# A list-scheduled transformer kernel: the first norm's small steps on VectorE, two routing steps for either engine, new lengths and due times in the layout

## The chip, the cores and the metric

The kernel runs on one core of a Trainium2 chip. That core has five engines with queues of their own: TensorE (matmul; PE in the profile, its weight loads PEld), VectorE (DVE), ScalarE (ACT), GpSimd (POOL) and SyncE (SP), which here only issues transfers. Each engine works through its own list of instructions in the order in which the program wrote them, and waits at semaphores for the others. The metric is the device time of one launch in microseconds; the time before is the median of three runs.

## What is computed

The reference is a stack of four gated layers over x of 16 batches x 128 tokens x 128 features, with a context of 77 rows a batch. Each layer adds a cross attention and a feed-forward part, each behind a layer norm and a tanh gate. Only what the change touches is shown in detail:

```python
def _layernorm(x, axis=-1, eps=1e-05):
    m = jnp.mean(x, axis=axis, keepdims=True)
    v = jnp.var(x, axis=axis, keepdims=True)
    return (x - m) / jnp.sqrt(v + eps)
...
    x = x + jnp.tanh(g_xattn[0]) * _L0_xattn_ref(_layernorm(x, axis=-1), ctx_1024, ctx_1024, ...)
    x = x + jnp.tanh(g_ffn[0]) * _L0_ffn_ref(_layernorm(x, axis=-1), L0_ffn_gate_w, L0_ffn_w1, L0_ffn_w2)
...
# layer 0's router, per token over E = 8 experts
select_prefix = jnp.arange(E)[None, :] <= k_idx[:, None]
R_sorted = jnp.where(select_prefix, p_sorted - rank, jnp.full_like(p_sorted, -1000000000.0))
...
tok_order = jnp.argsort(-R, axis=0)      # an expert keeps its 256 best tokens by R
```

Layers 0 and 1 attend with 16 heads of 8 features (layer 0 with a mask, and its weights are multiplied by a given matrix after the softmax), layer 2 with 16 heads of 64, layer 3 with 8 heads of 64. The feed-forward parts are a routed mixture of 8 experts, a dense layer with a second norm, a layer with 8-bit rounding, and a mixture that takes the best expert of each token.

## The kernel before

The tokens are worked on in four groups of four batches (`NG`, `GB`), a batch being 128 tokens on the 128 partitions. A group's x lies in SBUF throughout. Layer 0's attention goes group by group, eight units of half a batch each: scores on TensorE, the row maximum and the difference on VectorE (`less_max`, L632 and L634), exp on ScalarE (L839), the product with the given matrix on GpSimd or VectorE (`weighted`, L856), sums on VectorE (L844), transposes and the product with the values on TensorE. In layers 2 and 3 `weigh` (L995) takes the place of `weighted`.

**The order is laid out by a planner in the program.** Nothing is issued where it is written. Each piece of work is handed to `add(at, engine, cost, fn, reads, writes, new)`: a due time `at`, the engine or the engines that may do it, a cost in microseconds for each, and the keys it reads and writes. `Work.layout` (from L216) then runs a list scheduling over all pieces: whenever an engine is idle by its clock it takes the ready piece with the smallest due time. A piece that may go on two engines goes to the one that would finish it first by the costs, VectorE being charged 0.5 more (`SLACK`). The instructions are then written in this order, so costs and due times decide every engine's queue and nothing else. `NUDGES` (from L76) is a list of 582 triples: first piece, how many pieces, and hundredths of a microsecond added to their due times. `FLEX` is ScalarE or VectorE; `WEIGH` and `SIDE` are GpSimd or VectorE.

**The norm** (`norm`, L482) has five pieces: `stats` on VectorE (L491, four instructions), `moments` on GpSimd (L498 to L503, six instructions on 128x4 or 128x8 elements), `guess` on ScalarE (L508 and L510, logarithm and exponential), `newton` on GpSimd (L514 to L520, five instructions), and `scaled` on ScalarE (L526) or VectorE (L528), four instructions, one for each batch. `transposed` (L610) needs all four. The very first norm, of group 0 in layer 0, stands ahead of everything that TensorE does with x. At the start GpSimd also makes the identity, the head mask, `billion`, four cleared `vz` tiles (L1171) and the mask penalties `pen` (L1190, or on VectorE).

**Layer 0's routing** (`route_part`, L1525 to L1607) follows for each group once its logits are there: softmax, `before1` (L1562 to L1565) and `before2` (L1569 to L1577), which find an expert's rank and the mass ahead of it and make R from them, `spread` (L1582), which copies R sixteen times side by side, four transposes and their eviction into `RB`. All of its VectorE pieces were on VectorE alone. After the last group seven rounds of counting over `RB` (L1715) find each expert's cut.

Of the kernel before, what the change touches and what calls it, by code (L numbers as in the profile page):

```python
# [18 lines left out]
ALU = mybir.AluOpType  # L19
# [3 lines left out]
P = 128  # L23
B = 16
D = 128
SK = 77
NG = 4
GB = B // NG
GT = GB * P
GK = GB * SK  # L30
E = 8
# [28 lines left out]
WEIGH, WEIGH_COST = ("POOL", "DVE"), (1.3, 0.85)  # L60
SIDE, SIDE_COST = ("POOL", "DVE"), (1.3, 0.75)
# [12 lines left out]

NUDGES = (
    (206, 1, 230), (1755, 1, 143), (2153, 1, -200), (2640, 4, 268), (963, 1, -150), (960, 4, -257), (1701, 1, 117), (1797, 3,  # L76
    -30), (989, 1, -212), (1726, 8, -153), (2228, 4, 172), (2164, 2, -283), (1712, 1, -267), (1001, 1, -283), (1670, 6,
    -289), (1652, 1, -189), (813, 1, -237), (164, 8, -58), (162, 2, -260), (879, 6, 267), (1136, 1, -206), (141, 4, -145),
    (130, 1, 220), (738, 6, -165), (2242, 4, -104), (961, 1, -103), (2244, 8, -295), (1770, 2, 104), (488, 8, 333), (1339, 1,
    65), (466, 8, 69), (611, 4, 133), (1771, 1, -214), (65, 1, -226), (137, 4, -273), (2126, 1, -231), (567, 1, -156), (991,  # L80
    1, -231), (2046, 4, 47), (1919, 6, -283), (2452, 4, 299), (2195, 1, 100), (689, 1, -177), (1805, 2, 116), (332, 8, -352),
    (337, 8, -46), (956, 3, -22), (749, 8, -114), (2053, 8, 58), (2559, 1, -190), (501, 8, 217), (2655, 8, -72), (1935, 1,
    -263), (1015, 1, -100), (2403, 1, -88), (2766, 8, 120), (18, 8, 217), (399, 1, -14), (1548, 4, -46), (1542, 6, -252),
    (2445, 4, -44), (397, 8, 38), (849, 8, -70), (961, 1, -99), (1914, 2, -52), (1530, 4, -250), (869, 4, 264), (392, 1,
    156), (2068, 6, -52), (852, 4, 92), (1693, 2, -62), (991, 3, -232), (611, 8, 89), (869, 1, -276), (801, 1, 281), (2196,
    8, -30), (2416, 6, -273), (2216, 1, -248), (867, 5, -264), (2514, 5, -30), (798, 1, -157), (2351, 2, -317), (2685, 8,
    -69), (1474, 1, -91), (2385, 1, 256), (1690, 1, -24), (2175, 1, 121), (2054, 4, -47), (2514, 4, 127), (1485, 8, 274),
    (392, 2, 72), (2542, 6, -186), (1806, 8, 89), (987, 5, -196), (2633, 3, -250), (492, 8, -236), (406, 1, -183), (1838, 4,
    -210), (2352, 1, 274), (2199, 1, -277), (1610, 6, -212), (2547, 1, 242), (1723, 4, 60), (1676, 1, 271), (2059, 8, -270),
    (268, 8, -210), (1753, 8, 42), (2631, 2, -107), (1547, 1, -182), (1579, 4, 19), (377, 1, -73), (2080, 1, -38), (465, 1,  # L90
    -122), (2636, 3, 278), (995, 3, -161), (1571, 8, -123), (751, 1, -281), (249, 4, -311), (2634, 8, -121), (854, 6, 175),
    (798, 1, 75), (2614, 8, -397), (2289, 1, -240), (1009, 1, -99), (2536, 4, -99), (1299, 1, -270), (1024, 4, -270), (741,
    1, -114), (2480, 1, -296), (2417, 2, -257), (761, 1, -284), (2254, 2, -218), (971, 2, -251), (1011, 4, -314), (2837, 8,
    252), (1936, 4, 186), (2111, 8, -333), (1853, 1, 135), (600, 8, -33), (1839, 1, -241), (1855, 5, -100), (940, 1, -191),
    (769, 5, -205), (2002, 8, -31), (781, 4, -32), (756, 1, 62), (1072, 8, 12), (755, 2, -156), (2636, 2, 106), (1983, 8,
    -341), (1339, 1, -80), (1386, 1, -266), (859, 1, -136), (1416, 8, 137), (46, 4, 380), (756, 1, 143), (758, 1, -131),
    (1391, 2, 150), (2561, 1, -293), (940, 1, -187), (1841, 4, -270), (1507, 1, 86), (1946, 8, 10), (981, 1, -279), (446, 6,
    -301), (2680, 1, -210), (1864, 1, 190), (737, 2, -81), (1015, 1, 241), (1552, 3, 189), (2717, 4, -126), (18, 5, -237),
    (1001, 2, 288), (1022, 1, 163), (2195, 1, -59), (2536, 5, 258), (2458, 4, -80), (2490, 1, -296), (2494, 6, -198), (1560,
    4, -287), (1911, 5, -16), (864, 1, -297), (149, 3, 221), (1876, 4, 273), (1434, 4, -304), (2206, 3, -140), (41, 8, 260),  # L100
    (1443, 8, -98), (2206, 8, 75), (2039, 5, -256), (2046, 1, -229), (922, 1, -228), (985, 1, -170), (2074, 1, -269), (1418,
    4, -275), (2793, 5, -298), (2718, 4, -126), (1507, 1, -302), (869, 6, 233), (2206, 1, -48), (2034, 1, -65), (2068, 1,
    -220), (1851, 1, -301), (748, 4, 118), (1397, 8, 143), (1507, 1, 286), (1514, 1, -260), (375, 1, -253), (985, 1, -152),
    (2206, 1, -42), (2252, 1, -231), (1746, 8, 119), (2306, 1, 78), (1467, 6, -111), (1633, 1, 72), (1952, 1, -186), (981, 1,
    172), (411, 2, -92), (559, 8, 123), (397, 4, -18), (1219, 1, -151), (2480, 2, 127), (852, 1, -203), (1613, 2, 294),
    (2670, 8, -326), (2256, 1, -242), (953, 1, -194), (1058, 8, 100), (1952, 1, -49), (532, 1, -164), (1048, 4, -80), (1054,
    8, -91), (741, 1, -138), (2249, 8, 400), (987, 6, -205), (367, 6, -265), (803, 8, 294), (1414, 2, -267), (2897, 8, -243),
    (2492, 3, -282), (963, 1, 115), (1633, 1, -57), (1509, 1, -97), (1041, 2, 306), (806, 1, -238), (2008, 1, -88), (975, 1,
    -260), (920, 8, -208), (258, 8, -230), (491, 8, -48), (874, 1, -300), (607, 2, -81), (945, 1, -271), (789, 3, -171),
    (460, 1, 24), (791, 4, 298), (258, 2, 336), (741, 1, -71), (689, 1, -288), (2897, 4, 388), (1005, 1, -266), (959, 1,  # L110
    -21), (857, 1, 92), (431, 3, -191), (934, 1, -104), (801, 1, 296), (851, 4, -164), (854, 4, -222), (1851, 1, -94), (993,
    5, -152), (2101, 1, -233), (971, 1, 279), (972, 2, -204), (254, 1, -202), (1940, 8, -90), (869, 1, 75), (973, 1, -112),
    (1794, 3, -141), (2592, 4, -114), (973, 4, -248), (859, 6, -286), (2470, 1, -271), (1570, 2, -115), (533, 4, 282), (961,
    1, -279), (46, 8, -174), (969, 1, -122), (1612, 3, -61), (971, 2, -134), (2242, 5, 240), (2114, 8, -331), (1575, 4,
    -325), (2897, 4, -181), (2095, 4, -171), (276, 1, 275), (969, 1, -211), (1042, 1, -131), (1896, 4, 108), (969, 8, -121),
    (763, 1, -263), (2099, 3, -38), (2206, 4, -65), (1000, 4, -204), (2357, 4, 299), (579, 4, -325), (662, 3, -236), (2856,
    8, -367), (484, 8, 218), (2161, 1, -159), (223, 2, -98), (1570, 1, -262), (244, 8, -158), (222, 8, 52), (2175, 4, 50),
    (1503, 4, -114), (2473, 8, 89), (1843, 8, 137), (2215, 6, -274), (139, 1, 191), (1004, 6, -159), (748, 1, -271), (1838,
    4, -140), (2849, 1, 134), (999, 1, -226), (985, 4, -245), (2798, 5, -220), (922, 4, -286), (1052, 2, 119), (928, 5,
    -300), (981, 1, -222), (740, 8, -110), (1612, 4, -84), (1015, 2, -88), (996, 8, -105), (44, 8, -95), (2461, 5, 205),  # L120
    (1502, 4, -117), (2221, 4, -226), (485, 4, -357), (297, 4, -110), (1050, 4, -134), (2813, 1, -122), (1709, 1, -130),
    (1613, 8, 134), (2448, 8, 230), (969, 1, -243), (1004, 4, -257), (763, 1, -222), (2778, 4, 99), (2470, 8, 194), (689, 1,
    -221), (852, 4, -204), (741, 1, -194), (981, 1, -125), (1202, 6, -239), (894, 1, -144), (2159, 1, -243), (1609, 8, -138),
    (1466, 4, -384), (961, 1, -177), (991, 3, -168), (2474, 1, -277), (1057, 3, -180), (502, 1, -127), (2777, 5, 273), (1895,
    4, -78), (965, 5, -74), (995, 1, -230), (854, 4, -281), (154, 2, 382), (2206, 2, 85), (753, 2, -288), (2215, 6, -253),
    (969, 8, -361), (745, 4, 83), (974, 5, -239), (923, 6, -261), (983, 1, -186), (879, 1, 71), (625, 1, -169), (981, 1,
    -132), (140, 5, -185), (1802, 4, 47), (481, 8, 253), (2304, 2, -132), (1801, 5, -82), (2388, 6, 296), (743, 4, -136),
    (983, 6, 97), (872, 6, 146), (949, 5, -17), (865, 5, 90), (925, 5, -181), (136, 5, -180), (778, 1, -78), (803, 1, -263),
    (368, 1, 208), (2837, 8, 354), (1228, 1, 115), (2206, 1, -65), (1058, 1, -151), (793, 1, -302), (643, 1, 276), (2205, 3,
# [27 lines left out]
class Work:  # L157
# [50 lines left out]
    def nudged(self):  # L208

        due = [n["at"] for n in self.nodes]  # L210
        for first, count, hundredths in NUDGES:
            for i in range(first, min(len(due), first + count)):
                due[i] += hundredths / 100.0
# [1865 lines left out]
```

## Time and profile before

| what | us |
|---|---|
| median of three runs | 663.42 (663.17, 663.42, 665.4) |
| the profiled execution | 666.49 |
| its span, first to last instruction | 664.8 |
| L634 DVE difference, 112 instructions | 89.5 busy, 0.799 each |
| L632 DVE maximum, 112 | 87.4 busy, 0.780 each |
| L995 on POOL, 34 / on DVE, 14 | 1.216 / 0.899 each |
| L856 on POOL, 26 / on DVE, 6 | 1.387 / 1.031 each |
| L526 on ACT into xn, 92 / L528 on DVE, 20 | 0.486 / 0.551 each |
| L498 on POOL, 39 | 0.203 each |

The span lies inside the execution's time; what is around it is 1.7 us. An engine is busy while it computes; issuing transfers and waiting do not count. TensorE's mean granted clock is 0.976 of full speed. The kernel reads and writes 117.5 MB by DMA, at a mean of 177 GB/s.

### The profile page before, as it was taken

The page shows a single profiled execution, that of the slowest core. Times are in us where ns is not written, and L with a number is a line of the kernel's source. Part 1 is how long each engine was busy: PE and PEld are TensorE (multiplying, and loading weights), DVE is VectorE, ACT ScalarE, POOL GpSimd, SP SyncE. Part 2 cuts the span into 40 slices and gives each one's busy share as a digit, 9 for nine tenths or more (in the row PEclk, how much of TensorE's full clock was granted, in tenths as well). Part 3 has the DMA queues.
Part 4 walks back from the last instruction along what each step waited for, and adds up shares of the span by engine and source line. Part 5 has one row for each costly group of instructions (what it writes and reads, how often), then busy time and mean ns, then how long its engine had stood idle before and what let it go on. Part 6 is the DMA issues. An engine that isn't in the chain of part 4 may idle for free.

```text
span 664.8 us, 16370 instructions
## 1 busy us (share of the span) xinstructions
PE 604.2 (91%) x5795; PEld 435.4 (65%) x5795; DVE 524.9 (79%) x1224; ACT 427.2 (64%) x1131; POOL 305.8 (46%) x750
## 2 busy tenths in 40 slices
PE   3988998899999999988989999999999998799795
PEld 2555565565546778655646776687767776689795
DVE  3699999884675347999998998979999999878342
ACT  3545758577766656686687867647686758356463
POOL 8659445351000027624362735445445347645554
PEclk9888999999999999998999999999999999799898
DMA  8972473557445565489592757569964432666473
GB/s 228 272 233 68 150 183 110 150 165 207 144 131 159 160 187 144 140 239 296 160 269 88 217 169 227 188 175 315 292 178 130 122 98 83 198 180 181 125 225 84
DMA packets 169178, 117.47 MB, mean 177 GB/s; under 512 B 12649, under 2 KB 159984, under 8 KB 169098
## 3 DMA queue, kind: packets, MB, share of 16 engines
q1 hardware_dynamic: 166650, 112.55, 59.6%
q0 software_dynamic: 1728, 3.17, 1.3%
q8 instruction: 46, 0.75, 0.5%
q10 hardware_dynamic: 720, 0.71, 0.4%
q14 instruction: 34, 0.28, 0.1%
HBM read 61.43 MB, written 55.89 MB: 176 GB/s over the span
## 4 chain that ended last, share of the span: by engine, by line
PE 29%; DVE 13%; ACT 7%; POOL 7%; issue 2%; DMA 1%; another core or an unknown queue 1%; DVEq 0%; ACTq 0%; POOLq 0%
PE T L650 4%; PE h_ps L1927 4%; PE y L1001 4%; PE y L1942 3%; DVE pr L634 3%; PE q_ps L931 3%; DVE mx L632 2%; PE y L1062 2%; POOL pw L995 2%; PE h_ps L1041 2%; PE S L975 1%; DVE sb L988 1%; ACT xn L526 1%; PE O L885 1%; DVE ln_st L491 1%
## 5 line engine op out<-in xcount | busy, mean ns | idle before, releaser
L634 DVE TENSOR_TENSOR pr<-S,mx 128x616 f32<-128x616 f32 x112 | 89.5, 799 | 6.7
L632 DVE TENSOR_REDUCE mx<-S 128x8 f32<-128x616 f32 x112 | 87.4, 780 | 4.8 <-PE S L824 4.0
L650 PE MATMUL T<-ident,pw 128*128 128x128 f32 (+1 forms) x400 | 63.0, 284 | 6.5 <-POOL pw L995 4.3
L463 ACT COPY pT<-T 128x384 f32<-128x384 f32 x107 | 50.5, 479 | 26.6 <-PE T L650 26.0
L995 POOL TENSOR_TENSOR pw<-pr,rinv 128x616 f32<-128x616 f32 x34 | 41.2, 1216 | 53.5 <-DVE rinv L990 10.4
L650 PEld LDWEIGHTS T<-ident,pw 128*128 128x128 f32 (+1 forms) x400 | 45.9, 142 | 29.1 <-issue 12.0
L1001 PEld LDWEIGHTS y<-v,pT 128*128 128x128 f32 (+1 forms) x480 | 57.8, 191 | 9.6 <-issue 4.0
L1001 PE MATMUL y<-v,pT 128*128 128x128 f32 (+1 forms) x480 | 62.1, 278 | 1.5 <-ACT pT L463 1.1
L839 ACT ACTIVATE pr<-pr 128x616 f32<-128x616 f32 x64 | 45.9, 720 | 20.3 <-DVE pr L634 20.1
L856 POOL TENSOR_TENSOR pw<-pr,gp 128x616 f32<-128x616 f32 x26 | 36.0, 1387 | 37.2 <-ACT pr L839 23.9
L1811 DVE SCALAR_TENSOR_TENSOR token<-y,sc,token 128x128 f32<-128x128 f32 x96 | 32.9, 349 | 24.2 <-PE y L1806 21.7
L844 DVE TENSOR_REDUCE ss<-pr 128x8 f32<-128x616 f32 x64 | 49.6, 781 | 1.3 <-ACT pr L839 1.1
L931 PE MATMUL q_ps<-xT,wq 128*128 128x512 f32 x96 | 49.5, 613 | 0.8 <-DVE token L693 0.5
L463 ACT COPY vs<-f_ps 122x512 f32<-122x512 f32 (+3 forms) x57 | 33.1, 584 | 24.3 <-PE f_ps L1486 22.6
L1951 POOL DMA_INDIRECT out_x<-bo,row x30 | 29.8, 994 | 30.0 <-DVE bo L1946 15.1
L526 ACT ACTIVATE xn<-token,ln_b,ln_r 128x128 f32<-128x128 f32 x92 | 37.8, 486 | 7.4 <-POOL ln_b L520 7.3
L984 ACT ACTIVATE pr<-pr 128x616 f32<-128x616 f32 x48 | 34.0, 718 | 12.5 <-DVE pr L634 7.9
L657 ACT COPY pT<-T 128x128 f32<-128x128 f32 x104 | 28.2, 271 | 17.5 <-PE T L650 15.7
L1486 PE MATMUL f_ps<-vz,ctxT 128*122 128x512 f32 (+3 forms) x80 | 39.2, 602 | 0.1
L988 DVE TENSOR_REDUCE sb<-pr 128x8 f32<-128x616 f32 x48 | 37.4, 779 | 1.5 <-ACT pr L984 1.5
L975 PE MATMUL S<-k,q 64*64 64x77 f32 x1536 | 35.8, 235 | 0.9 <-DVE pr L634 0.8
L975 PEld LDWEIGHTS S<-k,q 64*64 64x64 f32 x1536 | 31.1, 136 | 7.7 <-issue 3.5
(338 smaller groups left out, 1490.4 us busy)
## 6 DMA issues: line engine op xcount, KB each, us to landing
v<-folded SPq DMA_DIRECT2D x48, 320.0 KB
vx<-apart SPq DMA_DIRECT2D x32, 320.0 KB
apart<-vz SPq DMA_DIRECT2D x32, 308.0 KB
rowsA<-blank SPq DMA_DIRECT2D x15, 516.0 KB
rowsZ<-blank SPq DMA_DIRECT2D x15, 516.0 KB
kept<-ks SPq DMA_DIRECT2D x24, 308.0 KB
k<-kept SPq DMA_DIRECT2D x12, 616.0 KB
folded<-vs SPq DMA_DIRECT2D x21, 308.0 KB
```

The lines of the kernel that those rows point to most:

```text
L463: nc.scalar.copy(out, src)
L526: nc.scalar.activation(o[:, i, :], src()[:, i, :], AF.Identity, bias=mem["b"][:, i:i + 1], scale=mem["r"][:, i:i + 1])
L632: nc.vector.tensor_reduce(mx, S4, axis=AX.X, op=ALU.max)
L634: nc.vector.tensor_tensor(pr.rearrange("p (a c) k -> p a c k", a=2), S4, mx.unsqueeze(3).to_broadcast([P, 2, 4, SK]), ALU.subtract)
L650: nc.tensor.transpose(own[jkey][:n, c, :], flat[:, lo:lo + n], ident)
L839: nc.scalar.activation(own["pr", i, half], own["pr", i, half], AF.Exp)
L844: nc.vector.tensor_reduce(own["s", i][:, 8 * half:8 * half + 8], own["pr", i, half], axis=AX.X, op=ALU.add)
L931: nc.tensor.matmul(own["q_ps", c], lhsT=wq()[:, (c0 + c) * P:(c0 + c + 1) * P], rhs=mem["xT"], start=True, stop=True)
L975: nc.tensor.matmul(S[rows64, a, c * SK:(c + 1) * SK], lhsT=own["q"][at, c, i * P + 64 * b:i * P + 64 * b + 64], rhs=own["k"][at, c, i * SK ...
L988: nc.vector.tensor_reduce(s, own["pr", i], axis=AX.X, op=ALU.add)
L995: eng.tensor_tensor(own["pw", i], own["pr", i], own["rinv", i].unsqueeze(2).to_broadcast([P, 8, SK]), ALU.mult)
L1001: nc.tensor.matmul(own["y", i], lhsT=own[u + (i, "pT", c // 3)][:n, c % 3, :], rhs=own["v", i][:n, c, :], start=(c == 0), stop=(c == 4))
```

## The change

Four things are done, in one diff.

The first norm (layer 0, group 0) gets `first=True`: its `moments` and `newton` run on VectorE with the same eleven instructions, and its scaling becomes two pieces of two batches each, one on ScalarE and one on VectorE; a piece without an instruction joins them. In all other norms only the costs change.

In `route_part` the second half of `before2` becomes a piece of its own, `before3`, which may run on GpSimd or VectorE, and so may `spread`. What were two instructions with a scalar and two tensors are three with one operation each, so that the piece has five instructions where there were four.

Costs in the layout are set anew for some pieces. The nudges are replaced as a whole, 597 in place of 582; 46 of them have a count of 0, which is a new form: it adds to the charge for taking the piece's second engine.

```diff
-WEIGH, WEIGH_COST = ("POOL", "DVE"), (1.3, 0.85)
-SIDE, SIDE_COST = ("POOL", "DVE"), (1.3, 0.75)
+WEIGH, WEIGH_COST = ("POOL", "DVE"), (1.25, 0.95)
+SIDE, SIDE_COST = ("POOL", "DVE"), (1.2, 1.2)
...
 NUDGES = (
...
@@ nudged, layout
-        due = [n["at"] for n in self.nodes]
+        due, odds = [n["at"] for n in self.nodes], [0.0] * len(self.nodes)
         for first, count, hundredths in NUDGES:
+            if count == 0:
+                odds[first] += hundredths / 100.0
             for i in range(first, min(len(due), first + count)):
                 due[i] += hundredths / 100.0
-        return due
+        return due, odds
...
+        second = [list(n["on"])[-1] for n in nodes]
+        slack = lambda i, e: SLACK.get(e, 0.0) + (odds[i] if e == second[i] else 0.0)
...
@@ norm
+        few = nc.vector if first else nc.gpsimd
...
-            nc.gpsimd.tensor_tensor(d, st[:, :, 1], st[:, :, 4], ALU.subtract)
+            few.tensor_tensor(d, st[:, :, 1], st[:, :, 4], ALU.subtract)
...
-        def scaled(e):
-            o = mem["o"] = out()
-            for i in range(GB):
+        def scaled(e, batches=range(GB)):
+            if "o" not in mem:
+                mem["o"] = out()
+            o = mem["o"]
+            for i in batches:
...
+        if first:
+            add(at, "DVE", 0.9, moments, writes=[ln])
+            act(at, 0.45, guess, writes=[ln])
+            add(at, "DVE", 0.7, newton, writes=[ln])
+            for n, e in enumerate(FLEX):
+                half = range(2 * n, 2 * n + 2)
+                add(at, e, 0.85, lambda e=e, half=half: scaled(e, half), reads=list(skeys) + [ln], writes=[okeys[0] + (n,)], new=() if n else new)
+            add(at, "NONE", 0.0, None, reads=[okeys[0] + (n,) for n in range(2)], writes=okeys)
+            return
...
-        add(at, FLEX, (1.6, 1.36), scaled, reads=list(skeys) + [ln], writes=okeys, new=new)
+        add(at, FLEX, (1.66, 1.75), scaled, reads=list(skeys) + [ln], writes=okeys, new=new)
...
-            add(at, FLEX, ((0.47, 0.55), (0.5, 0.45))[j], out, reads=[T], writes=[jkey])
+            add(at, FLEX, ((0.48, 0.55), (0.54, 0.55))[j], out, reads=[T], writes=[jkey])
...
-                    add(th + 0.1, ("POOL", "DVE"), (1.4, 0.85), weighted, reads=[prk, ("gp", g)], writes=[skey], new=[("pws", skey)])
+                    add(th + 0.1, ("POOL", "DVE"), (1.4, 1.15), weighted, reads=[prk, ("gp", g)], writes=[skey], new=[("pws", skey)])
...
@@ route_part
+        def before3(e):
+            eng = nc.gpsimd if e == "POOL" else nc.vector
+            rank, chosen = own["rank"], own["chosen"]
             R = f0["R"][:, gs, :]
-            nc.vector.scalar_tensor_tensor(R, rank, 1.0, pr(), op0=ALU.add, op1=ALU.subtract)
-            nc.vector.scalar_tensor_tensor(R, R, -1.0, chosen, op0=ALU.mult, op1=ALU.mult)
-            nc.vector.tensor_scalar(chosen, chosen, 1.0, 1e9, op0=ALU.subtract, op1=ALU.mult)
-            nc.vector.tensor_tensor(R, R, chosen, ALU.add)
+            eng.tensor_scalar(rank, rank, 1.0, None, op0=ALU.add)
+            eng.tensor_tensor(R, pr(), rank, ALU.subtract)
+            eng.tensor_tensor(R, R, chosen, ALU.mult)
+            eng.tensor_scalar(chosen, chosen, 1.0, 1e9, op0=ALU.subtract, op1=ALU.mult)
+            eng.tensor_tensor(R, R, chosen, ALU.add)
...
-        add(at, "DVE", 1.5, before1, reads=[key], writes=[key])
-        add(at, "DVE", 2.0, before2, reads=[key], writes=[key])
-        add(at, "DVE", 0.6, spread, reads=[key], writes=[kx], new=[("xn", kx)])
+        both = ("POOL", "DVE")
+        add(at, "DVE", 2.3, before1, reads=[key], writes=[key])
+        add(at, "DVE", 1.45, before2, reads=[key], writes=[key])
+        add(at, both, (1.2, 0.9), before3, reads=[key], writes=[key])
+        add(at, both, (0.9, 0.45), spread, reads=[key], writes=[kx], new=[("xn", kx)])
```

## The prediction

> **What bounds the kernel.** I read the page's first part, then busy time by stretch, then the timeline of the first 24 us, then the groups and timeline of the operations that the change touches.
>
> ```profile
> PE 604.2 (91%) x5795; PEld 435.4 (65%) x5795; DVE 524.9 (79%) x1224; ACT 427.2 (64%) x1131; POOL 305.8 (46%) x750
> ```
>
> TensorE is busy for 604.2 of 664.8 us, and the change takes no matmul away. So the question is what becomes of the 60.6 us in which TensorE idles. The next view is busy time in six stretches: start and end, length, then PE, PEld, DVE, ACT and POOL busy with their instruction counts, granted clock, DMA share, GB/s.
>
> ```profile
> 0.00:20.00 20.00, 8.66 (x24) 5.66 (x25) 6.51 (x21) 7.16 (x15) 17.16 (x55) 0.87 0.84 230
> 20.00:160.00 140.00, 126.23 (x1088) 79.72 (x1087) 125.12 (x264) 88.83 (x231) 73.30 (x136) 0.97 0.59 168
> 160.00:250.00 90.00, 90.00 (x371) 55.40 (x370) 47.57 (x121) 59.66 (x120) 7.14 (x24) 1.00 0.54 159
> 250.00:550.00 300.00, 285.32 (x3379) 206.97 (x3382) 274.85 (x583) 210.10 (x564) 144.22 (x409) 0.99 0.66 191
> 550.00:600.00 50.00, 41.28 (x491) 35.87 (x484) 41.45 (x128) 28.92 (x87) 29.92 (x70) 0.93 0.54 154
> 600.00:664.80 64.80, 52.67 (x458) 51.74 (x456) 29.38 (x110) 32.56 (x118) 34.05 (x62) 0.94 0.57 155
> ```
>
> TensorE's idle time is length less busy: 11.3 us before 20, 13.8 up to 160, none up to 250, 14.7 up to 550, 8.7 up to 600, and 12.1 at the end; 60.6 together. The reader is to see four regimes. At the start GpSimd is the full engine (17.16 of 20) while TensorE and VectorE wait. From 20 to 160 (layer 0's attention) VectorE is nearly full, 125.1 of 140. From 160 to 250 TensorE never stops. From 250 to 550 both are nearly full, 95% and 92%.
>
> The start, in order of time (start, length, engine, line, operation):
>
> ```profile
> 5.09 0.87 DVE L491 BATCH_NORM_STATS2 ln_st<-token 128x6 f32<-128x128 f32 x4 [5.09 <-DMA token<-in_x]
> 5.26 3.63 POOL L1171 MEMSET vz<- 128x1024 f32 x4
> ...
> 8.86 0.21 POOL L498 TENSOR_TENSOR ln_d<-ln_st 128x4 f32<-128x4 f32 x1
> ...
> 9.38 1.43 DVE L766 TENSOR_TENSOR kx<-ks,headmask 128x1232 f32<-128x1232 f32 x1
> 9.46 1.42 POOL L501 TENSOR_SCALAR ln_w<-ln_sq 128x4 f32<-128x4 f32 x1
> ...
> 12.67 1.50 POOL L514 TENSOR_TENSOR ln_t<-ln_r 128x4 f32<-128x4 f32 x1
> ...
> 15.32 1.65 ACT L526 ACTIVATE xn<-token,ln_b,ln_r 128x128 f32<-128x128 f32 x4 [3.28 <-POOL ln_b L520]
> ...
> 15.87 1.63 PE L610 MATMUL tp<-ident,xn 128*128 128x128 f32 x4 [4.88 <-ACT xn L526]
> ```
>
> The statistics are ready at 5.96, but GpSimd first clears vz and starts on them only at 8.86. Two of its four-column steps last 1.42 and 1.50 us where the other norms need 0.19 and 0.20, each under a VectorE kx of 1.43. The mask pen stands between them on GpSimd from 11.43 to 12.69. So xn is finished at 16.97, and VectorE meets its first score (L632) at 23.07. Before that VectorE has done only 7.6 us of work (2.37 up to 10, 4.13 up to 20, then 0.75 and 0.31).
>
> **Part A, the first norm.** Removed from GpSimd: 6 + 5 small steps. Added to VectorE: the same 11. Rows: routing's small steps of 128x32 (L1574 to L1577) last 0.18 to 0.19 and follow each other every 0.22 us. So ln_w is ready at 5.96 + 5 x 0.22 = 7.1. The guess on ScalarE (0.44 from 11.19 to 11.63) must wait for a table load that ends at 7.47, so r is there at 7.9. Five steps more, 1.1, and a hop: 9.1. Scaling is four pieces of 0.41 on ScalarE (1.65); now two there and two on VectorE at 0.34 (L528's median), side by side 0.85. So xn is done at 10.0 instead of 16.97: 7.0 earlier on the path. The wait for r now stands in VectorE's queue; behind it are the vz evictions (L788), the bias rows and kx, and kx is what the scores also need. VectorE's own load bounds the gain again: 7.6 us of earlier work plus 11 x 0.22 + 0.7 = 3.1 makes 10.7, which from 5.09 ends no sooner than 15.8, against 23.07: at most 7.3. The other end is 0: the landing times of the masks and of vx aren't shown, and DMA is busy at 0.84 of its share here. Against that end, vx is issued at 15.11 and first used at 29.71 with no wait seen. I take -5.5, nearer to the two bounds that agree on 7 than to 0, because kx and the vz evictions must share VectorE with the norm. Is an earlier start kept? Layer 0 is bound by VectorE, whose list from there on is unchanged, and the full TensorE of 160 to 250 only moves up with it. So yes, unless a transfer is late next.
>
> **Part B, routing steps.** Two steps of each group may go to GpSimd: R's last arithmetic (now five instructions, four before) and its spread.
>
> ```profile
> 76.50 1.66 DVE L1562 TENSOR_TENSOR tie<-r_pr 128x256 f32<-128x256 f32 x1
> ...
> 81.64 0.19 DVE L1577 TENSOR_TENSOR R<-R,chosen 128x32 f32<-128x32 f32 x1
> 81.74 0.35 DVE L693 SCALAR_TENSOR_TENSOR token<-y,tg,token 128x128 f32<-128x128 f32 x1
> 82.00 0.42 DVE L1582 COPY rx<-R 128x512 f32<-128x512 f32 x1
> ```
>
> On VectorE they cost 4 x 0.22 + 0.42 = 1.3 a group. Groups 0 to 2 lie in VectorE's full stretch, so at most 3.9 is saved. Group 3's (at 175) lies under the full TensorE and is worth nothing unless that cover goes. On GpSimd nothing of this form ran: its norm steps follow every 0.28 (L515 to L520), 5 x 0.28 = 1.4, and a 128x512 pass is 1.18 (L689), so 2.6, 1.3 more latency before the transposes; if group 3's is uncovered, +1.3. GpSimd has 73.3 of 140 busy, so its queue takes the step, but a weighting (L856, 1.39) may stand behind it. The fifth instruction adds 0.22 where VectorE keeps the step. I take -1.0, between -3.9 and +1.3, since the layout moves a step only where it expects VectorE to finish later.
>
> The row of tie above shows a price of such moves: 1.66 us against 0.42 in the other groups, just while GpSimd's L856 runs from 76.49 to 77.88. The Trainium skill, "SBUF — State Buffer", section "Who interferes with whom", says that a VectorE instruction with two SBUF inputs and a GpSimd instruction that reads SBUF take turns on a shared port pair for the whole instruction. As an estimate by that rule, every moved step can hold VectorE for its own length, 3 x 2.6 = 7.8 against 3.9 saved, so that the part would read +3.9 instead of -1.0 and the total 660.8.
>
> **Part C, the measured lengths.** They shift the choice of engine: VectorE's weighting becomes dearer (0.85 to 0.95 and to 1.15), its side passes 0.75 to 1.2, its scaling 1.36 to 1.75. The rows agree: L995 on VectorE has a mean of 0.899, L856 1.031, L528 0.551 a piece. Work that can leave: L995 12.6, L856 6.2, L528 9.8, side passes 2.8, 31.4 us in all on VectorE. It goes to engines with room (ScalarE 210 of 300, GpSimd 144 of 300 between 250 and 550) but lasts longer there: 1.22 for 0.80 on L995. The gain is bounded by TensorE's idle time, which is owed to many causes; the loss by latency, 14 x 0.42 = 5.9. I take -1.0, range -6 to +5.9: nearest is the row that says TensorE already runs at 95% there.
>
> **Part D, the due times.** All 582 nudges go and 597 others come, some of them on the choice of engine. The trace can't price an order that it doesn't contain. Bounds: all of TensorE's 14.7 idle us between 250 and 550 gone, or that whole stretch at the rate of its first 100 us (4.0 + 6.1 idle, so 30.5): +15.8. I take 0.
>
> The sum is -5.5 - 1.0 - 1.0 + 0 = -7.5. The profiled execution took 666.49 with a span of 664.8, so 1.7 lie around the span; the span should come to 657.3 and that execution to 659.0. Carried to the median of the runs, 663.42 (3.1 below the profiled execution), this is 655.9.
>
> **Rivals.** First, more than that: the truer lengths halve the idle time between 250 and 550, 7.3 more, 648.6. For it: VectorE's 92% there, so a lighter VectorE is felt. Against: the chain of waits there alternates between TensorE, VectorE and the others, and no wait stands out. Second, a start that is hidden anyway: DMA share 0.91 from 10 to 40 holds masks or vx back, A is 0, and 661.4 is left, no change that shows. For it: that share. Against: no TensorE wait on a transfer between 6.5 and 600. Third, slower: the new order makes the L1 to L3 stretch, 250 to 550, wait for GpSimd's longer passes; at the rate of its first 100 us it costs +15.8, so 671.7. It cancels all gains from +7.5 and shows as a loss from +10.8. For it: TensorE's transposes already wait 4.3 us for GpSimd's pw, and the old order is fitted to these queues. Against: that engine is half idle.
>
> **How the numbers follow.** Forecast 0.47, the larger gain 0.18, hidden start 0.15, slower order 0.20. Faster by over 0.5% (under 660.1) is 0.65, within 0.5% 0.15, slower (over 666.7) 0.20; half a per cent is about what runs of this kernel can tell, 663.17 to 665.4. The forecast's own range is 651 to 660. The range for 8 in 10 reaches to the larger gain's value less a little, 646, and into the slower case, 668.
>
> **What would show it.** A: L498 to L520 on VectorE before 10, the first xn transposes near 10 to 11, the first L632 near 17 to 18, no 4.9 us TensorE wait for xn. B: rx and R's steps on GpSimd in groups 0 to 2. C: fewer than 14 L995, 6 L856 and 20 L528 instructions on VectorE, its busy sum below 520. D: TensorE idle between 250 and 550 near 14.7. The prediction is wrong if the first L632 is not before 21, or if the early start is there and idle time of 250 to 550 or of the end grows by more than it.

## The result and the profile after

| what | before | after |
|---|---|---|
| median of 6 runs each | 663.61 | 660.25 (656.95 to 661.19) |
| ratio, 95% interval | | 0.994 [0.9913, 0.9967] |
| the same kernel again, 12 runs | 663.47 | 661.19, ratio 0.998 [0.9958, 1.0002] |
| profiled execution / its span | 666.49 / 664.8 | 661.02 / 659.3 |

The change gains 2.3 to 3.4 us by the medians; 7.5 had been forecast. The two profiled spans differ by 5.5, more than the medians, because the profiled execution of before was 2.9 above its median and that of the changed kernel 0.8. The stretches of the changed kernel, in the columns of the table of before:

```profile
0.00:20.00 20.00, 11.36 (x42) 6.63 (x42) 11.27 (x35) 7.62 (x16) 17.03 (x55) 1.00 0.84 221
20.00:160.00 140.00, 131.38 (x1097) 83.62 (x1097) 123.46 (x264) 90.94 (x232) 83.08 (x151) 0.98 0.64 178
160.00:250.00 90.00, 89.88 (x376) 54.83 (x375) 46.95 (x118) 56.33 (x110) 9.53 (x15) 1.00 0.56 166
250.00:550.00 300.00, 283.83 (x3423) 206.73 (x3424) 275.93 (x596) 206.35 (x556) 153.03 (x435) 0.99 0.65 188
550.00:600.00 50.00, 44.41 (x438) 38.55 (x437) 42.35 (x139) 27.34 (x80) 31.01 (x60) 0.90 0.52 148
600.00:659.30 59.30, 48.42 (x428) 47.05 (x426) 25.26 (x92) 29.43 (x107) 32.47 (x59) 0.97 0.59 160
```

Length less TensorE's busy time: 8.6 idle in the first stretch (11.3 before) and 8.6 in the second (13.8), but 16.2 between 250 and 550 (14.7), then 5.6 up to 600 (8.7) and 10.9 at the end (12.1). The same operation can lie in another stretch after the change, so its start in both traces says more: the first row maximum is 3.8 earlier, the first counting round 6.6 (171.3 against 177.9), layer 3's first logits 4.5 (552.9 against 557.4). In these two traces the gain is made before 180, and part of it is given back between 180 and 553. VectorE's sum is 525.2 (524.9 before): it was not relieved. GpSimd's is 326.2 (305.8).

The start of the changed kernel, in order of time (start, length, engine, line):

```profile
6.09 0.17 DVE L507 TENSOR_TENSOR ln_d<-ln_st 128x4 f32<-128x4 f32 x1
...
6.38 1.66 DVE L510 TENSOR_SCALAR ln_w<-ln_sq 128x4 f32<-128x4 f32 x1
...
8.50 0.20 ACT L519 ACTIVATE ln_r<-ln_lg 128x4 f32<-128x4 f32 x1
...
10.34 0.15 DVE L523 TENSOR_TENSOR ln_t<-ln_r 128x4 f32<-128x4 f32 x1
...
11.32 0.88 ACT L537 ACTIVATE xn<-token,ln_b,ln_r 128x128 f32<-128x128 f32 x2 [2.21 <-DVE ln_b L529]
11.32 0.60 DVE L539 TENSOR_SCALAR xn<-token,ln_r,ln_b 128x128 f32<-128x128 f32 x2
...
19.23 0.80 DVE L652 TENSOR_REDUCE mx<-S 128x8 f32<-128x616 f32 x1 [2.15 <-PE S L844]
```

The reader is to see two losses. ln_w, a step of four columns, takes 1.66 us. And the guess is ready at 8.70, but the Newton step begins at 10.34, because values, query bias and mask stand ahead of it in VectorE's queue. So xn is done at 12.20 (forecast 10.0), and the first row maximum (now L652) starts at 19.23 instead of 23.07: 3.8 earlier, not 5.5.

A routing part of the changed kernel, group 0's:

```profile
75.54 1.67 POOL L876 TENSOR_TENSOR pw<-pr,gp 128x616 f32<-128x616 f32 x1 [3.42 <-issue]
75.99 1.50 DVE L1585 TENSOR_TENSOR before<-before,tie 128x256 f32<-128x256 f32 x1
...
78.04 0.53 POOL L1600 TENSOR_SCALAR rank<-rank 128x32 f32<-128x32 f32 x1 [0.82 <-DVE rank L1589]
...
80.30 0.61 POOL L1609 COPY rx<-R 128x512 f32<-128x512 f32 x1
```

Five small instructions and the spread now run on GpSimd, from 78.04 to 80.91, 2.87 us against the 2.6 worked out. They do so in groups 0, 1 and 3; group 2's stayed on VectorE (its spread at 150.2 is 0.426 long, where GpSimd needs 0.609). Groups 0 to 2 had been forecast.

### The profile page after: what moved, and what is told of

The parts are those of the page before. It is cut to its first block, busy times and chain, and to the rows that moved or that the text cites. A ratio compares the mean times of both kernels' runs of the same rounds, so it can differ in the third digit from the quotient of the medians.

```text
span 659.3 us, 16387 instructions
## 1 busy us (share of the span) xinstructions
PE 609.3 (92%) x5795; PEld 437.4 (66%) x5795; DVE 525.2 (80%) x1241; ACT 418.0 (63%) x1095; POOL 326.2 (49%) x773
## 4 chain that ended last, share of the span: by engine, by line
PE 29%; DVE 12%; POOL 7%; DMA 3%; issue 3%; ACT 2%; POOLq 0%; DVEq 0%; SPq 0%
PE y L1021 5%; PE T L670 4%; PE q_ps L951 4%; PE y L1082 2%; PE S L995 2%; POOL out_x L1980 2%; DVE pr L654 2%; DVE mx L652 2%; PE h_ps L1061 2%; PE h_ps L1956 2%; PE y L1971 1%; DVE sb L1008 1%; PE O L905 1%; DMA row<-rowsZ 1%; PE h_ps L1120 1%
## 5 line engine op out<-in xcount | busy, mean ns | idle before, releaser
L652 DVE TENSOR_REDUCE mx<-S 128x8 f32<-128x616 f32 x112 | 87.6, 782 | 5.7 <-PE S L844 3.9
L1015 POOL TENSOR_TENSOR pw<-pr,rinv 128x616 f32<-128x616 f32 x41 | 50.0, 1225 | 71.1 <-DVE rinv L1010 33.9
L470 ACT COPY pT<-T 128x384 f32<-128x384 f32 x99 | 46.6, 481 | 23.0 <-PE T L670 22.5
L876 POOL TENSOR_TENSOR pw<-pr,gp 128x616 f32<-128x616 f32 x28 | 39.2, 1401 | 25.5 <-ACT pr L859 15.2
L951 PE MATMUL q_ps<-xT,wq 128*128 128x512 f32 x96 | 48.1, 605 | 0.7 <-ACT xT L470 0.7
L677 ACT COPY pT<-T 128x128 f32<-128x128 f32 x97 | 26.7, 275 | 26.8 <-PE T L670 26.4
L470 ACT COPY vs<-f_ps 122x512 f32<-122x512 f32 (+3 forms) x56 | 32.8, 585 | 16.9 <-PE f_ps L1506 16.2
L537 ACT ACTIVATE xn<-token,ln_b,ln_r 128x128 f32<-128x128 f32 x86 | 35.3, 487 | 6.2 <-POOL ln_b L529 4.0
L995 PE MATMUL S<-k,q 64*64 64x77 f32 x1536 | 36.0, 235 | 0.4 <-DVE pr L654 0.4
L995 PEld LDWEIGHTS S<-k,q 64*64 64x64 f32 x1536 | 31.1, 136 | 7.6 <-issue 3.2
```

Of the source, the lines that this page charges most:

```text
L470: nc.scalar.copy(out, src)
L652: nc.vector.tensor_reduce(mx, S4, axis=AX.X, op=ALU.max)
L951: nc.tensor.matmul(own["q_ps", c], lhsT=wq()[:, (c0 + c) * P:(c0 + c + 1) * P], rhs=mem["xT"], start=True, stop=True)
L995: nc.tensor.matmul(S[rows64, a, c * SK:(c + 1) * SK], lhsT=own["q"][at, c, i * P + 64 * b:i * P + 64 * b + 64], rhs=own["k"][at, c, i * SK ...
L1015: eng.tensor_tensor(own["pw", i], own["pr", i], own["rinv", i].unsqueeze(2).to_broadcast([P, 8, SK]), ALU.mult)
```

## The experiments

The experiments ran on three chips, with the kernel before beside each: its medians were 668.55 on the first (norm_on_pool, route_on_dve, old_due, start_more), 663.47 and 663.55 on the second, and 662.95 on the third (norm_on_pool2). Ratios are to the runs beside them. A ratio need not carry from one chip to another: one and the same kernel, norm_on_pool below, has 0.9965 on the first and 1.0005 on the third, and the two intervals only just overlap. "Landmarks" are the starts of the same operations in two traces (the first maximum, the counting rounds, layer 3's logits and so on).

**Parts undone in the changed kernel's own order.** Engines are swapped after the layout, so the order of the queues stays.

```diff
-        few = nc.vector if first else nc.gpsimd
+        few = nc.gpsimd
```

> The changed kernel with its order of work untouched; only the eleven small steps of the first norm are issued on GpSimd again (its scaling stays halved). Theory, the gain is the earlier start carried to the end: the first score maximum goes from 19.2 back to 22.5 to 24 and the whole time rises by about the same, to 663 to 665. Rival, the gain comes from the new layout and the start is absorbed later: the first maximum is late, but the time stays at 660, within 1.

Measured: 665.86, ratio 0.9965 [0.9944, 0.9985], on the chip where before took 668.55. Most landmarks are 3.0 to 3.4 later than in the changed kernel, the first maximum (22.4) by 3.1 and layer 3's first logits by 3.0; layer 1's first feed-forward product only by 2.0. The shift is carried to the end (span 663.1 against 659.3). The changed kernel itself did not run on that chip, so the median was taken again:

> norm_on_pool once more (the changed kernel in its own order, the eleven small steps of the first norm back on GpSimd), since on its first chip the kernel before took 668.55 and the changed kernel itself was not run there. If the parts are as the traces say (first maximum 3.2 later, carried to the end), it takes 3 to 4 us more than the changed kernel's 661.19: 664 to 665, ratio to before 1.001 to 1.003 on a chip where before takes 663.5. Rival: the ratio of the first chip, 0.9965, holds here too (661.2); then the norm's steps are worth nothing that a median shows, and all of the 5.6 us between the changed kernel and order_alone belongs to the routing steps.

Measured: 664.39, ratio 1.0005 [0.9979, 1.003], 3.2 over the changed kernel's 661.19 (1.7 by the ratios' difference of 0.0025). In its start the chain waits in GpSimd's queue as in the kernel before:

```profile
9.56 0.59 POOL L510 TENSOR_SCALAR ln_w<-ln_sq 128x4 f32<-128x4 f32 x1
...
13.70 0.19 POOL L523 TENSOR_TENSOR ln_t<-ln_r 128x4 f32<-128x4 f32 x1
...
22.80 0.80 DVE L652 TENSOR_REDUCE mx<-S 128x8 f32<-128x616 f32 x1 [1.98 <-PE S L844]
```

The guess is done at 10.92; the Newton step starts only at 13.70. First maximum 22.80 against 19.23, counting rounds 174.8 against 171.3, layer 3's first logits 556.3 against 552.9: 3.4 to 3.6. Against the second trace of the changed kernel (171.9 and 553.4) the last two are 2.9. TensorE's granted clock is no rival here: it rose from 0.87 to 1.00 in the first 20 us with the change, but it is 1.00 in norm_on_pool2 too. So the norm's steps on VectorE are worth about 3.3 us in this order. The halved scaling stays in all of these kernels; what it is worth by itself was not run.

```diff
-            eng = nc.gpsimd if e == "POOL" else nc.vector
+            eng = nc.vector
...
-            (nc.gpsimd if e == "POOL" else nc.vector).tensor_copy(own["rx"], ...)
+            nc.vector.tensor_copy(own["rx"], ...)
```

> The changed kernel with its order untouched; the last arithmetic of R and its spread are issued on VectorE in all four groups, also where the layout meant GpSimd. Theory, these moves are worth nothing or little: 659.5 to 661.5. Rival, they relieve a full VectorE by up to 3.9 us between 20 and 160: 662 to 664. Second rival, the shared port made them a loss: 657 to 659.

Measured: 667.23, ratio 0.9964 [0.9942, 0.9987]. First maximum 18.8 (19.2 in the changed kernel); the counting rounds start 2.3 later, layer 3's logits 3.5 (1.7 and 3.0 against the second trace of the changed kernel). The trace says 1.7 to 3.5 us for these steps; the ratio alone could not tell it. With both edits at once:

> The changed kernel in its own order, with the first norm's small steps back on GpSimd and the two routing steps back on VectorE: what the new lengths and due times bring without the moved steps. norm_on_pool (0.9965 on its chip) lost 3.3 us at the first maximum against the changed kernel and route_on_dve 2 to 3 us from the tied ranks on. If the parts add up, both together lose 4 to 6 us: ratio to before 1.000 to 1.004, so lengths and due times alone are worth nothing. Rival: lengths and due times carry part of the gain: ratio 0.994 to 0.998.

Measured: 666.81, ratio 1.0056 [1.0036, 1.0075]. The changed kernel took 661.19 on the same chip, so **the moved steps together are worth 5.6 us in this order** (5.0 by the ratios), more than the whole change gains. Against norm_on_pool2 it is 2.4 by the medians and 3.4 by the ratios; that would be the routing steps, but it compares two chips. Against the kernel before beside it, it is 3.3 slower: **the new order without the moved steps is a loss**, and the rival (0.994 to 0.998) is out. That is not yet the price of the new lengths and due times by themselves. The halved scaling is still in, and the order was laid out for steps that are now elsewhere; an order laid out anew without them was not run. Nor does a trace show where the 3 us go: the counting rounds start at 175.7 against 177.9 before, layer 1's first feed-forward product at 308.3 against 312.3, layer 3's first logits at 557.3 against 557.4. The profiled execution of before was 3 us above its median and this one 2 below, so the loss is in the medians alone.

**The due times.** The changed kernel with the 582 old nudges, carried to the same pieces:

```diff
 NUDGES = (
-    (the 597 new triples)
+    (the 582 old triples, numbered for the new pieces)
 )
```

> The changed kernel (norm, routing pieces, lengths) with the 582 due-time nudges of the kernel before, each put on the same piece as there. Theory, the nudges only fit the pieces and costs that they were found with: the start stays early (first maximum at 18.5 to 20.5), TensorE idles more from 20 on, 668 to 685. Rival, the due times are worth nothing, the start is all: 659 to 661.5.

Measured: 690.63, ratio 1.0333 [1.0303, 1.0363], 22 us slower, with the first maximum at 18.0, earlier than in any of the parts above. Its last two stretches:

```profile
550.00:600.00 50.00, 35.65 (x506) 29.46 (x506) 43.68 (x112) 25.66 (x68) 23.98 (x65) 0.90 0.36 104
600.00:686.80 86.80, 71.94 (x586) 69.31 (x584) 39.03 (x147) 44.22 (x157) 44.52 (x83) 0.91 0.59 157
```

TensorE idles 14.4 of 50 us, then 14.9 of 86.8. The early start is there and the end is not. The loss builds up on the way: against the changed kernel the counting rounds are 2.6 later (173.9 against 171.3), layer 3's first logits 15.2 (568.1 against 552.9). Here the due times did not suit another set of pieces and lengths. The time did not change with one nudge less, though:

> The changed kernel without the last of its 597 nudges (-0.31 us on four pieces from number 1004 on); the layout takes no other engine anywhere and differs only in the place of some pieces. Theory, the due times matter as a set that fits, single ones little: within 0.3% of the changed kernel. Rival, the order is so finely tuned that any change costs: 0.5% or more slower.

Measured: 661.20, ratio 0.9978 [0.9958, 0.9998]. In its profiled execution ln_w took 3.00 us and the first maximum came at 20.18, 1.0 later than in the changed kernel. Beside it, the changed kernel itself on the same chip:

> The changed kernel as it is, on the same chip as the three below, so that spans can be set beside each other. Both theories: ratio to the kernel before 0.991 to 0.997, the first score maximum at 19.2.

Measured: 661.19, ratio 0.998 [0.9958, 1.0002].

**More of the start.** Is an earlier first maximum always kept? The finished order of the changed kernel was edited by a list of moves, "this piece right behind that one", with nothing laid out anew; and ln_w became one two-input instruction.

```diff
-            few.tensor_scalar(mem["w"], sq[:, :, 1], 4.0 / D, 4.0 * EPS, op0=ALU.mult, op1=ALU.add)
-            few.tensor_tensor(mem["w"], mem["w"], d, ALU.add)
+            few.scalar_tensor_tensor(mem["w"], sq[:, :, 1], 4.0 / D, d, op0=ALU.mult, op1=ALU.add)
...
+        for moved, behind in MOVES:       # newton and the scaled halves right behind the guess, queries ahead of group 1's keys
+            order.remove(moved)
+            order.insert(order.index(behind) + 1, moved)
```

> The changed kernel, same layout, with the first norm's chain moved up by hand: newton and the two scaling pieces stand right behind the guess, ahead of the vz evictions in VectorE's queue, the queries ahead of group 1's keys, and the variance is made by an instruction of two tensor inputs instead of the one that lasted 1.66 us; 1e-5 is added in newton and no longer before the guess. Theory, an earlier start is kept to the end: first maximum at 16.5 to 18 and 658 to 659.5 in all. Rival, something else is late next (vx, the masks, kx): first maximum early, time 660 to 661.5.

Measured: 664.46, ratio 0.9933 [0.9899, 0.9967]. xn was done at 10.34, near the forecast's 10.0, but the first maximum came at 19.75: the transposes stood behind v_ps, which waited for ScalarE's ks, and group 1's keys and values stood between queries and scores. The next moves put ks ahead of the scaling and the scores ahead of group 1:

> As start_more, but the first keys are copied out on ScalarE before the halves of xn, and the first scores stand ahead of group 1's keys and values in TensorE's queue, which held them up there. Theory, an earlier start is kept to the end: first maximum at 15.5 to 17.5, every later landmark up to the last layer-3 score 1.7 to 3.5 earlier than in the changed kernel, ratio to it 0.994 to 0.998. Rival, group 1 is late next or the transfers hold it: landmarks from 60 on as in the changed kernel, ratio 0.999 to 1.003.

Measured: 664.27, ratio 1.0013 [0.9986, 1.0039]. The first maximum (L669 in this kernel) is later, not earlier:

```profile
17.00 1.41 PE L861 MATMUL S<-kx,qs 32*128 32x308 f32 x8
...
19.95 1.44 DVE L803 TENSOR_TENSOR kx<-ks,headmask 128x1232 f32<-128x1232 f32 x1 [5.76 <-ACT ks L799]
...
21.70 0.79 DVE L669 TENSOR_REDUCE mx<-S 128x8 f32<-128x616 f32 x1
```

The scores are done at 18.41, but VectorE's queue holds group 1's kx, whose keys TensorE now makes after the scores. VectorE waits 5.76 us in front of work that it could do. So in the third kernel group 1's kx and values went behind the maximum, and the mask's matmuls ahead of the transposes. (It leaves out one dependence: the copy of group 1's first values to `apart` now stands ahead of the instruction that writes them to `vz`, and copies what the tile held before.)

> The changed kernel; as in start_more2 the first norm's steps follow one another at once and the small constant of the variance enters in the Newton step (after the guess); now also the mask's eight matmuls of the first scores stand ahead of the transposes of xn, and group 1's copied keys and values stand behind the first maximum in VectorE's queue. In start_more2 the first scores were done at 18.4 and the first maximum began at 21.70, because VectorE's queue held group 1's copied keys (19.95 to 21.39, waiting for ScalarE's ks) ahead of it. If that queue was the cause, the first maximum now begins at 17.0 to 18.0 (changed kernel: 19.23). If an earlier start is kept, all later landmarks and the end follow by 1 to 2 us: 658 to 660, ratio to before about 0.993 on a chip where before takes 663.5. Rival: below 19 something else decides (group 1's scores, its keys now late): no gain or a loss of 1 to 3 us, ratio 0.996 to 1.002.

Measured: 666.67, ratio 1.0047 [1.0025, 1.0069].

```profile
15.18 0.80 DVE L671 TENSOR_REDUCE mx<-S 128x8 f32<-128x616 f32 x1 [1.86 <-PE S L870]
...
20.40 1.65 ACT L554 ACTIVATE xn<-token,ln_b,ln_r 128x128 f32<-128x128 f32 x4 [1.43 <-POOL ln_b L546]
...
21.68 0.47 SPq L845 DMA_DIRECT2D apart<-vz  x1
...
21.95 0.70 ACT L885 ACTIVATE pr<-pr 128x616 f32<-128x616 f32 x1
...
26.72 0.68 DVE L840 TENSOR_TENSOR vz<-v_ps,rows 77x128 f32<-77x128 f32 x3 [8.57 <-issue]
...
27.32 0.79 DVE L671 TENSOR_REDUCE mx<-S 128x8 f32<-128x616 f32 x1
```

The first maximum is at 15.18, 4 us ahead of the changed kernel and earlier than I had expected. Yet the second maximum is at 27.32 (20.98 in the changed kernel). VectorE waits 8.57 us ahead of group 1's values. The profile's view names no releaser, but the wait's own record lasts from 16.02 to 26.67, and of the two semaphores that it waits for the later one is that of the misplaced copy, issued at 21.68 and landed at 26.64. The first exp on ScalarE waits too, for group 1's xn, which GpSimd brings no sooner than 20.40. The second maximum is 6.3 after the changed kernel's, and nearly every later landmark 6.4 to 7.5 (the counting rounds at 178.8 against 171.3, layer 3's first logits at 559.9 against 552.9). So this kernel shows what a copy in the wrong place costs, and is no clean test of the theory that the kernel follows its first maximum.

**The norm alone.** The kernel before, with the first norm on VectorE and two engines for its scaling, its chain moved up by hand, nothing laid out anew:

```diff
-        add(at, FLEX, (1.6, 1.36), scaled, ...)
+        add(at, FLEX, (1.6, 1.36), halves if first else scaled, ...)     # halves: two batches on ScalarE, two on VectorE
...
+        for moved, behind in MOVES:
```

> The kernel before with its order of work, in which only the first norm is put on VectorE (eleven steps, halved scaling) and its chain up to the first scores is moved up by hand; no new lengths, no new due times, no routing on GpSimd. Theory, the start is most of the change's gain: first maximum at 16 to 18.5 against 23.1, 3 to 6 us less in all, ratio 0.991 to 0.9955. Rival, the start is lost on the way and the new order brought the gain: ratio 0.997 to 1.002.

Measured: 666.97, ratio 1.0068 [1.0042, 1.0094]. xn was done at 11.6, the scores at 18.48, and the first maximum started at 23.17 against 23.07: VectorE's queue held group 1's kx, values and mask ahead of it, and the mask's transfer landed at 22.94. With the whole way of group 0 moved up as one piece:

> The kernel before, with the first norm's steps on VectorE and its scaling on two engines, and no new due times; the first group's way (keys, mask, values, transposes, queries, scores, first maximum) moved ahead by hand as one piece. In norm_alone the first scores were done at 18.48, but the first maximum began at 23.17, behind group 1's keys, values and mask (that one waits for its transfer until 22.94) in VectorE's queue. If that was the cause, the first maximum now begins at 17 to 18.5 instead of 23.07. Theory 'the whole kernel follows the first maximum': end 4 to 6 us earlier than before, ratio 0.992 to 0.994. Rival 'the rest of the order has to be planned for it': the other landmarks of group 0 and 1 don't move, because the engines' queues behind the first maximum still hold group 1's norm (done on GpSimd near 24) ahead of group 0's next steps: ratio 0.998 to 1.003.

Measured: 669.75, ratio 1.0102 [1.0075, 1.013].

```profile
18.87 0.80 DVE L647 TENSOR_REDUCE mx<-S 128x8 f32<-128x616 f32 x1 [2.14 <-PE S L839]
...
26.74 1.65 ACT L537 ACTIVATE xn<-token,ln_b,ln_r 128x128 f32<-128x128 f32 x4 [1.77 <-POOL ln_b L529]
...
29.43 0.72 ACT L854 ACTIVATE pr<-pr 128x616 f32<-128x616 f32 x1
```

The first maximum is 4.2 earlier than before, the first exp 4.7 later (24.74 before): ScalarE's queue has group 1's xn in front, and that norm, on GpSimd, is now later. Nearly all later landmarks are 7 us behind before's. The rival was right in kind and too mild in size. **The theory that the kernel follows its first maximum falls here.** It follows the queues behind it. The hand-moved orders that ran on the changed kernel's chip are all slower than it (664.27, 666.67, 666.97 and 669.75 against 661.19). start_more ran on the first chip, where the changed kernel did not, so their medians can't be set beside each other; its counting rounds (172.7) and layer 3's first logits (554.0) are 0.6 to 1.4 later than in the two traces of the changed kernel.

## Why the prediction was right in its sign and too large

The first measurement, 660.25, lies in the range for 8 in 10 (646 to 668) and just outside the forecast's own range (651 to 660); "under 660.1", which had 0.65, was missed by a little. The gain was half of the forecast or less.

**Part A (-5.5): mis-sized, -3.3.** The mechanism held: L507 to L529 run on VectorE, the 4.88 us wait of TensorE for xn is down to 1.99, and the gain at the first maximum is kept to the end when the order behind it was laid out for it (norm_on_pool2). The -3.3 is that of the moved steps; the halved scaling, which was part of A too, was not measured. The step that failed is "6 + 5 small steps at 0.22 each". It took the price of a step from routing rows that ran without GpSimd's clearing of vz beside them, and the wait in VectorE's queue as nothing: ln_w took 1.66 us, and ln_m and the bias rows 0.8 each (0.41 and 0.27 in norm_alone2), and the Newton step stood 1.6 us in the queue. The text had named "the wait for r now stands in VectorE's queue" but looked only at what is behind it, not at what the norm would itself stand behind. start_more shows that removing both brings xn to 10.34, so the 10.0 was right for the chain alone; but then other queues hold the first maximum at 19.75, so in that order the difference of 1.7 was not had by shortening the norm.

**"Is an earlier start kept? Yes, unless a transfer is late next."** Kept, yes, in the planned order. The premise that VectorE's list is unchanged from there on does not hold, since the change lays every list out anew. And the condition was too narrow: in start_more2 and the two norm_alone kernels it was mostly group 1's work in VectorE's and ScalarE's queues that was late next, and once a transfer (the mask at 22.94).

**Part B (-1.0): right in sign, larger in size.** Between norm_on_pool2 and order_alone lie 2.4 us by the medians, 3.4 by the ratios, and 1.0 at layer 3's first logits by the traces, although order_alone's first maximum was 1.1 the earlier one; route_on_dve's trace says 1.7 to 3.5. The bounds were -3.9 and +1.3. That the steps take longer on GpSimd (2.87) cost nothing that these runs show.

**The rule of the Trainium skill weighed there** ("SBUF — State Buffer", section "Who interferes with whom"): the turns it describes are in the trace, 1.50 us instead of 0.42 for `before` (L1585) while GpSimd's product runs 1.67 instead of its mean of 1.40. They already were there before (tie, 1.66). Beside the moved steps of group 0 (0.25 to 0.53 each) VectorE's instructions keep their usual lengths, 0.42 and 0.43 for 128x256. The estimate of +3.9 for this part was not met.

**Parts C and D (-1.0 and 0): the gain did not come.** With the moved steps taken out, the new order is 3.3 us slower than before (order_alone), where -1.0 had been forecast; what C and D are worth beside the moved steps is not shown. C's own signs were mixed. L995's successor went from 14 to 7 on VectorE and L856's from 6 to 4, as forecast, but the scaling rose from 20 to 26 and VectorE's sum stayed at 525 where "below 520" was forecast. For D the idle time of 250 to 550 stood at 16.2, near the 14.7 forecast. The trace could not price the order, as the text said; a loss of 3.3 lies well inside the bounds given. Which of lengths and due times costs it stays open: the old due times on the new pieces were 22 us slower than before, and the new ones with the old lengths were not run.

So -3.3 and -2.4 for the moved steps and +3.3 for the order stand where -7.5 was forecast, and for the measured -2.3 on that chip (-3.4 in the first measurement). These three are steps from one median to the next, so that they meet the measured sum by themselves; that is no check of them. Firm is their one comparison on a single chip, 5.6 for the moved steps together. Luck had a part in how near A and B came together (5.6 against 6.5): A was forecast too large and B too small. The sign held because 5.6 is more than the 3.3 of the order. **The rivals:** the larger gain did not come. "A start that is hidden anyway" (661.4) is near the time, but for another reason: A is worth 3.3, and the order takes that away. The slower order is real in order_alone, at 3.3 instead of 15.8.

## What to carry to other kernels

In this kernel, whose queues are laid out in advance, a shorter chain was worth what the queues behind it could take up. Before pricing a moved step, list what stands ahead of it on its new engine, and what of the next group stands ahead of its consumer. After changing pieces, lengths and due times together, undo the parts one at a time in the new order, so that the moved steps and the new order are priced apart, and set the kernels beside each other on one chip. Here the steps gained 5.6 us in the new order, and that order without them was 3.3 slower than the old one. When an order is edited by hand, look in the trace for each copy's issue behind the write that feeds it (21.68 and 26.72 in start_more3).

## What the runs showed of the hardware

While GpSimd clears vz in four instructions (from 5.28 to 8.92 in the changed kernel), VectorE's instructions with one tensor and a scalar are long and its two-input ones are not. ln_w on 128x4 as TENSOR_SCALAR took 1.66 us in the changed kernel's first trace, 1.89 in its second, and 1.69 to 3.00 in five other kernels. In six of these seven it ends within 0.05 us of the end of one of the four clears; in one_nudge_less, with 3.00, it ends 0.3 after the last. Two-input steps of the same size at 6.03 to 6.43 in start_more2 took 0.16 or 0.17; one that stood behind such a TENSOR_SCALAR (rows, 1.47) took 1.27 and ended with it. The Trainium skill, in the section named above, says both: that tensor_scalar can enter a mode that locks the port pair against GpSimd, when its operands meet certain conditions, and that a two-input instruction doesn't contend with one that only writes. The lengths agree; the mode itself is not seen in a trace.

Part of the spread within a kernel goes with the granted clock: twelve runs of order_alone go from spans of 662.8 to 668.0, with mean clocks of 0.977 or more up to 666.0 and 0.970 to 0.975 in the three longest. It is not a strict rule: the kernel before, beside it, had a span of 663.6 at 0.985 and one of 661.7 at 0.971. So a single trace against a single trace can be off by some microseconds in its end: the two first profiles were 5.5 apart, where the medians were 3.4. The two traces of the changed kernel differ by 0.6 at the counting rounds (171.3 and 171.9) and by 1.1 at the first exp (20.89 and 21.95), so small terms need medians of many runs.
